# A four-layer graph network on one core: VectorE operations split at 512 columns on gathered tiles, and a rearranged start for the first graph

## The chip, the core and the metric

The kernel runs on one core of one Trainium2 chip. The metric is device time in microseconds, from 14 runs of the kernel before: median 3405.66, lowest 3397.34, highest 3418.8. One further execution was recorded by the profiler; all durations in the text come from that one.

## The reference

There are 16 graphs of 1024 nodes with 64 features each. `adj` is a weighted adjacency matrix (1024 x 1024, about one entry in 128 set, plus the diagonal), `nodemask` a flag for each node. Four layers run one after the other on the features `x`, each on a normalised input and with its result added to `x`:

```
h = max(layernorm(x), 0)
0: x += (adj @ h) @ W^T
1: m = relu(relu(h W1 + b1) W2 + b2);  msg = relu(adj @ m);  x += GRU(msg, h)
2: T0 = h, T1 = adj @ h, T2 = 2 adj @ T1 - T0;  x += (sum of K_k T_k) Wc + bc
3: neighbours = adj > 0; rows of more than 10 neighbours (where the mask is set) drop every skip-th one, in both directions
   agg = 0.25 q(0.25) + 0.5 q(0.5) + 0.25 q(0.75), each q a quantile over the neighbours' h, feature by feature
   x += (relu((h + agg) M1 + mb1) M2 + mb2) * mask
```

## The kernel before

Only the class `Fast` runs on these inputs; a second path (`general_kernel`) is there for inputs that it cannot hold. Engines are called by letters in the code: `T` is TensorE (PE), `V` VectorE (DVE), `S` ScalarE (ACT), `G` GpSimd (POOL), `D` SyncE (SP). All operations of the main part are recorded through one helper, so most of them show as L301 in the profile; the gathers are L622, stores through SP L628, scatters L1288.

**Tiles.** Nodes of a graph lie on 128 partitions in 8 blocks (`NT` = 8), so a feature tile is 128 x 512 in fp32, a block of the adjacency matrix 128 x 8 x 128 (512 KB). `pay` holds for each node x, the normalised h, its list of neighbours, counts and its mask; `G` holds up to 11 gathered neighbours per node (its own row and 10 more), `net` the scratch of the sorting network; there are two `G` buffers and one `net`.

**Chains.** The work is written as generators ("chains") that yield one operation at a time:

- `transposing` (L845): loads blocks of `adj` by SP, transposes them on PE, copies them to `AT` tiles on ACT. There are 15 `AT` tiles, 8 per graph. The first graph's eight blocks are loaded at the start, six of them into parts of the `G` buffers, which are not yet in use.
- `coding` (L652): signs of the `AT` tiles on ACT (`there`, fp16), the diagonal cleared on DVE, and a product on PE with powers of two, which packs a node's neighbours into code words.
- `listing` (L635): loads the node mask, casts and transposes it once; then for each graph turns code words into lists of neighbours with MAX8 and MATCH_REPLACE on DVE (`cand`, `L`, `hit`), and applies the dropping rule.
- `layering` (two chains, even and odd graphs): `layers` (L895) with layers 0 to 2, and the fourth norm. `norm` (L879) sums a row of x on DVE (`st`), takes eight squares with accumulation on ACT (`sq`, `va`), a root on ACT (`sd`), a reciprocal and an offset on DVE (`ri`, `off`), and eight ReLUs with scale and offset on ACT. The product of layer 0 (`into`) follows on PE, block by block. At the end the list goes into `pay` ("pay fill"), the fourth norm writes its h, and SP stores `pay` in DRAM: as `table` (h alone, for the gathers) and as `rows`.
- `gathering`: for each graph 80 indirect DMAs issued by POOL (10 neighbours x 8 blocks, 128 rows each) into a `G` buffer. After graph 16 four more groups follow, for nodes with more neighbours (`MANY`: 1, 2, 4 and 2 blocks of 128 nodes with 23, 15, 13 and 13 entries).
- `quantiling`: on the gathered tile, marks repeated entries (`hits`, `bad`), adds 1e30 to them, sorts with min/max networks (`tensor_tensor` on `G` and `net`), and weighs the wanted places with `coef`.
- `dense`: the sum of the weighed places and the last two products on PE, the mask on DVE (`yo`), the store of the output.

**The width of a VectorE operation.** A network step acts on several places at once. `quantiles` cuts it so that no operation has more than `LONGEST` = 1024 columns: with T = 8 blocks and C = 64 features a place has 512 columns, so `few` is 2 places. The mask addition and the multiplication by `coef` are cut in the same way.

```python
few = max(1, int(LONGEST / (T * C)))

def parts(k):
    count = -(-k // few)
    return [slice(k * i // count, k * (i + 1) // count) for i in range(count)]
```

**The order.** A planner (`Weave.run`, L440) gives every operation an estimated cost (`Line.cost`, L304) and issues, at each step, on the engine that can start earliest, the ready operation of the chain with the lowest key. The keys make graph b's transposes (b - 2.5) and layers (b - 3) run ahead of its lists (b - 1.5), gathers and quantiles (b + 1). The order on each engine is then fixed as a dependence from one instruction to the next, so each engine runs its instructions in the planner's order, whatever their real times are. A change of any operation or cost therefore can change the order of all that follows.

Of the kernel before, what the change touches and what calls it, by code (L numbers as in the profile page):

```python
# [16 lines left out]
AF = mybir.ActivationFunctionType  # L17
ALU = mybir.AluOpType
AX = mybir.AxisListType
# [3 lines left out]
P = 128  # L23
N = 1024
NT = N // P
# [76 lines left out]
GATHER = 1.33  # L102
RANK = 3.0
SHARE = 3
LONGEST = 1024
AT = 15
LIST_KEY = -1.5
CODE_KEY = -2
# [177 lines left out]
class Line:  # L286
# [15 lines left out]
        return op  # L302

    def cost(self, method, out, reads, kwargs):  # L304
        n = max(a.free_size() for a in [out] + reads)
        extra = "accum_out" in kwargs
        if self.name == "DVE":
            fixed = {"match_replace": 0.27, "max": 0.16}.get(method, 0.155)
            return fixed + n / 960 + 0.08 * extra, 0.0
        if self.name == "ACT":  # L310
            scalars = sum(hasattr(kwargs.get(k), "ap") for k in ("bias", "scale"))
            return 0.225 + n / 1400 + 0.09 * scalars + 0.19 * extra, 0.0
        if self.name == "PE":
            if method == "transpose":
                return 0.12, 0.25
            n = out.free_size()
            if n == NB and mybir.dt.size(reads[0].dtype) == 2:
                return 0.12, 0.3
            pair = n == 512 and reads[0].shape[0] == P and out.shape[0] == C
            return (0.46 if pair else max(0.22, 0.06 + n / 545)), 0.3  # L320
        if self.name == "SP":
            return 0.4, 2.0 + out.nbytes() / 150e3
        return 1.33, 2.2


class Weave:
# [16 lines left out]
    def give(self, name, t):  # L343
        self.stocks[name].append(t)
# [121 lines left out]
class Fast:  # L466
# [4 lines left out]
    def __init__(self, tc, half, whole, weights):  # L471
# [93 lines left out]
        self.weave = weave = Weave(tc)  # L565
        self.T, self.V, self.S = Line("PE", nc.tensor), Line("DVE", nc.vector), Line("ACT", nc.scalar)
        self.G, self.D = Line("POOL", nc.gpsimd), Line("SP", nc.sync)
        self.take = {}
        weave.leash = None, None

# [64 lines left out]
    def listing(self, nodemask):  # L635
        V = self.V
        mf, mu8 = self.small("h1", (P, 512))[:, 0:P], self.small("h1")[:, P:2 * P].bitcast(U8)[:, 0:P]
        yield self.D.dma_start(mu8, nodemask.rearrange("b (t p) -> (b t) p", p=P))
        yield V.tensor_copy(mf, mu8)
        bank = yield "q"  # L640
        yield self.T.transpose(bank[:, 0:P], mf, self.ident)
        self.mask = self.small("mask", (P, P))
        yield V.tensor_copy(self.mask, bank[:, 0:P])
        self.weave.give("q", bank)
        for b in range(GRAPHS):
            yield float(b) + LIST_KEY
            yield from self.lists(b)
        yield float(GRAPHS) - RANK
        yield from self.longest()

    def coding(self):

        V, T, S = self.V, self.T, self.S
        for b in range(GRAPHS):
            yield float(b) + CODE_KEY
            bank = yield "bits"
            yield T.matmul(bank.rearrange("p (t w) -> p t w", w=NB), self.ones16[0:1, 0:P],
                           self.low[0:1, None, :].to_broadcast([1, NT, NB]), start=True, stop=False)
            turned = self.turned[b]
            for j in range(0, NT, 2):  # L660
                there = yield "there"
                for i in range(2):
                    yield lambda: len(turned) > j + i
                    yield S.activation(there[:, i, :], turned[j + i], AF.Sign)
                self.masked[b] = j + 2
                own = there.rearrange("p i (t m) -> p (i t) m", m=P)[:, j:j + NT + 2:NT + 1, :]
                yield V.tensor_mul(own, own, self.noteye[:, None, :].to_broadcast([P, 2, P]))
                for i in range(2):
                    for t in range(NT):
                        yield T.matmul(bank[:, t * NB:(t + 1) * NB], there[:, i, t * P:(t + 1) * P],  # L670
                                       self.bits[:, (j + i) * NB:(j + i + 1) * NB], start=False,
                                       stop=j + i == NT - 1 and t == NT - 1)
                self.weave.give("there", there)
            code = yield "code"
            yield S.activation(code.rearrange("p t w -> p (t w)"), bank, AF.Copy, scale=1.0 / UNIT)
            self.weave.give("bits", bank)
            self.coded[b] = code
# [167 lines left out]
    def transposing(self, adj):  # L845

        D, T, S = self.D, self.T, self.S
        blocks = {}


        early = self.early

        def load(i):
            b, j = divmod(i, NT)
            blocks[i] = block = early.pop(0).rearrange("p (t m) -> p t m", m=P) if 2 <= i < NT else (yield "block")
            yield D.dma_start(block, adj[b, :, j * P:(j + 1) * P].rearrange("(t p) m -> p t m", p=P))

        total = GRAPHS * NT
        yield -1.0
        for i in range(NT):  # L860
            yield from load(i)
        for i in range(total):
            b, j = divmod(i, NT)
            yield float(b) - 2.5
            if NT <= i + 1 < total:
                yield from load(i + 1)
            block = blocks.pop(i)
            at = yield "AT"
            for half in range(2):
                bank = yield "tp"  # L870
                for q in range(4):
                    yield T.transpose(bank[:, q * P:(q + 1) * P], block[:, 4 * half + q, :], self.ident)
                yield S.activation(at[:, 512 * half:512 * half + 512], bank, AF.Copy)
                self.weave.give("tp", bank)
            if not 2 <= i < NT:
                self.weave.give("block", block)
            self.turned[b].append(at)

    def norm(self, w, h, X, then=None):  # L879

        V, S = self.V, self.S
        st, va, sd, ri, off = (self.small(f"{name}{w}") for name in ("st", "va", "sd", "ri", "off"))
        yield V.tensor_reduce(st, X, axis=AX.X, op=ALU.add)
        yield V.tensor_scalar(st, st, -1.0 / C, None, op0=ALU.mult)
        sq = self.small(f"sq{w}", (P, C))
        for t in range(NT):
            yield S.activation(sq, X[:, t, :], AF.Square, bias=st[:, t:t + 1], accum_out=va[:, t:t + 1])
        yield S.activation(sd, va, AF.Sqrt, bias=self.eps, scale=1.0 / C)
        yield V.reciprocal(ri, sd)
        yield V.tensor_mul(off, st, ri)  # L890
        for t in range(NT):
            yield S.activation(h[:, t, :], X[:, t, :], AF.Relu, bias=off[:, t:t + 1], scale=ri[:, t:t + 1])
            if then:
                yield from then(t)

    def layers(self, w, b, x):
# [10 lines left out]
        def into(bank, h, last=False):  # L907

            def step(j):
                if j == 0:  # L910
                    yield lambda: len(turned) > 0
                yield lambda: len(turned) > j
                for half in range(2):
                    yield T.matmul(bank[half * C:(half + 1) * C, :], h[:, j, :], turned[j][:, cols[half]],
                                   start=j == 0, stop=not last and j == NT - 1)
                if last:
                    yield lambda: self.masked[b] > j
                    give("AT", turned[j])
            return step
# [10 lines left out]

        h = yield "nodes"
        bank = yield "fm"
        yield from self.norm(w, h, X, into(bank, h))
        self.turns += 1
        wide = yield "wide"
        aggT = wide[0:C, :]
# [15 lines left out]
        def turn(t):  # L952
# [3 lines left out]
            if t % 4 == 3:  # L956
                yield S.activation(cat[0:C, cols[t // 4]], turned_h[-1][0:C, :], AF.Copy)
                give("fm", turned_h[-1])
        yield from self.norm(w, h, X, turn)
        aug = yield "wide"  # L960
        for half in range(2):
            bank = yield "fm"
# [57 lines left out]

        h = yield "nodes"
        bank = yield "fm"
        yield from self.norm(w, h, X, into(bank, h))
        wide = yield "wide"
        t1 = wide[0:C, :]
        for half in range(2):
# [21 lines left out]
                yield T.matmul(both[half * C:(half + 1) * C, t * P:(t + 1) * P], h[:, 4 * half + t, :], self.k02,  # L1048
                               start=False, stop=t == 3)
        give("nodes", h)  # L1050
        aug = yield "wide"
        for half in range(2):
            yield S.activation(aug[0:C, cols[half]], both[half * C:(half + 1) * C, :], AF.Copy)
        give("fm", both)
        bank = yield "fm"
        o = yield from by_node(bank, aug[0:C, :], self.wca, self.bcr)
        give("wide", aug)
        yield V.tensor_add(X, X, o)
        give("fm", bank)


        yield lambda: b in self.listed
        L, notes = self.listed[b]
# [6 lines left out]
                              op0=ALU.mult, op1=ALU.add)  # L1070
        give("L", L)
        give("notes", notes)
        yield from self.norm(w, pay[:, :, H:H + C], X)
        table = self.table[b * STRIDE:b * STRIDE + N, :].rearrange("(t p) c -> p t c", p=P)
        yield self.store(b, "table", table, pay[:, :, H:H + R])
        rows = self.rows[b * N:(b + 1) * N, :].rearrange("(t p) w -> p t w", p=P)
# [870 lines left out]
```

## Time and profile before

| | us |
|---|---|
| median of 14 runs | 3405.66 (3397.34 to 3418.8) |
| the profiled execution | 3409.64 |
| its span (first to last recorded work) | 3407.7 |
| busy: PE | 1783.7 (52%) |
| busy: VectorE | 1548.1 (45%) |
| busy: POOL | 1432.6 (42%) |
| busy: ACT | 1095.1 (32%) |
| first gather starts | 161.2 |
| gathers of graphs 1, 2, 3, 4 (from 0) start | 352.1, 552.8, 745.5, 930.7 |
| gather of the last graph starts | 3035.1 |
| the four groups after it | 3156.2 to 3362.8 |

The mean granted clock of TensorE was 0.656. No engine is busy for more than 52% of the span, so the bound is not read from busy shares; one has to see which engine waits for which, stage by stage. In the page's second part each digit is the busy share of one fortieth of the span (85 us) in tenths. In the part with groups, a line gives the source line, engine, operation, output <- inputs and count, then the busy time and the mean of one in ns, then the idle time of that engine just ahead of these operations and what ended most of it. A line of waits gives the idle time in total, how often, and the longest. On the timelines, consecutive operations of one name are put together: start, time, and "x3" for three; shapes are those of the row. SPq and POOLq are the sequencers, where DMA issues show. In a table of windows each engine's busy time and count stand for one stretch, then the granted clock, the DMA engines' share and the GB/s.

### The profile page before, as it was taken

How to read it: one execution, taken by the hardware profiler on the slowest of the kernel's cores; microseconds unless marked ns; L12 is line 12 of the kernel's file. 1: busy time of each engine (PE TensorE's matmuls, PEld its weight loads, DVE VectorE, ACT ScalarE, POOL GpSimd, SP SyncE). 2: the span in 40 equal slices, each digit the busy share in tenths (PEclk: the TensorE clock that was granted, in tenths of full speed). 3: DMA queues.
4: the chain of work that ended last, by engine and by line, in shares of the span. 5: the costliest groups of instructions: out<-in, count | busy, mean ns of one | idle time of the engine just before them, and what ended most of it. 6: DMA issues, size and time to landing. Idle time of an engine off the chain costs nothing. (4 is left out here: it accounts for less than half of the span.)

```text
span 3407.7 us, 24102 instructions
## 1 busy us (share of the span) xinstructions
PE 1783.7 (52%) x7024; PEld 818.6 (24%) x7024; DVE 1548.1 (45%) x3675; ACT 1095.1 (32%) x3002; POOL 1432.6 (42%) x1441
## 2 busy tenths in 40 slices
PE   6727355382736547282836646581836666433222
PEld 3302112140313223131413212230412232111121
DVE  2212136271725436271725436371725436395846
ACT  5503324160515234151614224250614334111100
POOL 1070623517071634526170634426061534437674
PEclk8857568575777667585767666575766667655555
DMA  3211322222212212222312112221212221112110
GB/s 83 60 27 49 46 43 52 35 63 27 62 31 54 45 30 61 31 51 30 75 25 52 39 31 51 45 58 25 69 25 39 41 38 25 18 21 28 24 29 15
DMA packets 246841, 141.00 MB, mean 41 GB/s; under 512 B 76048, under 2 KB 223952, under 8 KB 246704
## 3 DMA queue, kind: packets, MB, share of 16 engines
q1 hardware_dynamic: 199824, 90.21, 11.0%
q0 software_dynamic: 46096, 48.62, 10.6%
q8 instruction: 59, 0.97, 0.1%
q10 hardware_dynamic: 784, 0.57, 0.1%
q14 instruction: 78, 0.64, 0.1%
HBM read 120.12 MB, written 19.17 MB: 41 GB/s over the span
## 5 line engine op out<-in xcount | busy, mean ns | idle before, releaser
L622 POOL DMA_INDIRECT G<-table,pay x1402 | 1401.0, 999 | 1923.0 <-DVE net L301 1185.9
L301 PE MATMUL bank<-AT,nodes 128*64 128x512 f32 x2048 | 624.7, 691 | 118.6 <-issue 65.9
L301 PE MATMUL bank<-G,c 128*128 128x512 f32 (+3 forms) x382 | 202.5, 653 | 158.6 <-DVE G L301 158.2
L301 PE MATMUL bank<-wide,wg 64*64 64x512 f32 (+1 forms) x192 | 121.9, 721 | 301.7 <-ACT wide L301 301.6
L301 PEld LDWEIGHTS bank<-AT,nodes 128*64 128x64 f32 x2048 | 161.2, 154 | 428.7 <-issue 306.0
L301 PE MATMUL bank<-c,block 128*128 128x128 f32 x976 | 234.2, 371 | 18.1 <-ACT AT L301 8.2
L301 ACT ACTIVATE wide<-bank 64x512 f32<-64x512 f32 x128 | 75.7, 591 | 477.9 <-remote 340.4
L301 DVE MAX8 L<-cand 128x8 f16<-128x103 f16 x384 | 92.3, 263 | 275.1 <-remote 178.4
L301 PE MATMUL bank<-of_h,m 64*128 64x512 f32 (+2 forms) x72 | 62.3, 960 | 280.6 <-issue 227.1
L301 ACT ACTIVATE sq<-pay,st 128x64 f32<-128x64 f32 x512 | 177.7, 347 | 93.3 <-DVE st L301 78.2
L301 ACT ACTIVATE AT<-bank 128x512 f32<-128x512 f32 x256 | 150.2, 590 | 164.5 <-PE bank L301 116.6
L301 PEld LDWEIGHTS bank<-c,block 128*128 128x128 f32 x976 | 155.9, 190 | 171.1 <-issue 140.2
L301 DVE TENSOR_TENSOR G<-G 128x1024 f32<-128x1024 f32 (+7 forms) x215 | 187.4, 902 | 2.2
L301 DVE TENSOR_TENSOR hn<-nodes,bank 128x256 f32<-128x256 f32 x32 | 13.4, 419 | 378.6 <-remote 297.4
L301 DVE SCALAR_TENSOR_TENSOR of_h<-bank,bhn,wide 64x512 f32<-64x512 f32 x32 | 23.8, 744 | 351.3 <-PE bank L301 197.4
L301 PE MATMUL bank<-m,h 128*128 128x64 f32 x274 | 69.0, 410 | 203.6 <-ACT h L301 179.6
L301 ACT ACTIVATE nodes<-pay,off,ri 128x64 f32<-128x64 f32 x384 | 153.5, 429 | 26.8 <-DVE off L301 16.2
L301 DVE TENSOR_TENSOR net<-G 128x1024 f32<-128x1024 f32 (+7 forms) x140 | 140.4, 1032 | 3.2 <-PE bank L301 2.1
L301 PEld LDWEIGHTS bank<-G,c 128*128 128x128 f32 x382 | 74.1, 240 | 272.9 <-issue 150.4
L301 ACT ACTIVATE G<-G,coef 128x64 f32<-128x64 f32 x384 | 95.2, 336 | 127.9 <-DVE coef L301 127.9
L301 ACT ACTIVATE there<-AT 128x1024 f16<-128x1024 f32 x128 | 132.4, 1045 | 0.4
L301 PEld LDWEIGHTS bank<-m,h 128*128 128x128 f32 x274 | 59.7, 308 | 256.0 <-ACT h L301 190.8
(188 smaller groups left out, 2631.0 us busy)
## 6 DMA issues: line engine op xcount, KB each, us to landing
block<-in_adj SPq DMA_DIRECT2D x122, 512.0 KB
G<-table,pay POOLq DMA_INDIRECT x1402
rows<-pay SPq DMA_DIRECT2D x16, 632.0 KB
table<-pay SPq DMA_DIRECT2D x16, 264.0 KB
pay<-in_x SPq DMA_DIRECT2D x16, 256.0 KB
out<-yo SPq DMA_DIRECT2D x16, 256.0 KB
G<-in_adj SPq DMA_DIRECT2D x6, 512.0 KB
c<-in_half ACTq DMA_DIRECT2D x1, 246.0 KB
```

Source lines behind the costliest of these rows:

```text
L301: return Op(self, lambda: f(*args, **kwargs), writes, reads, cost, later)
L622: return self.nc.gpsimd.indirect_dma_start(out=out, out_offset=None, in_=table, in_offset=bass.IndirectOffsetOnAxis(ap=at, axis=0))
```

## The change

Six things are changed.

1. `LONGEST` is 512, so `few` is 1 for the 16 graphs: mask, network and coefficient operations have at most 512 columns. The instructions on VectorE rise from 3406 to 3984 in the built program.
2. A second name for ACT's queue, `self.A`; the odd-numbered blocks of the first graph are loaded by ACT, the even-numbered ones by SP. The planner's cost of a DMA goes by the operation and no longer by the engine.
3. The cast of the node mask waits until the first graph is coded.
4. The coding of words waits until the first graph's product of layer 0 has been issued (`turns > 0`).
5. `norm` has a second form, used for the first graph's four norms: the rows are centred on VectorE, squared and reduced there, the root stays on ACT, and one VectorE operation does the ReLU and the scaling. The eight squares and the eight ReLUs on ACT go (32 and 32 in four norms).
6. For all graphs, the pay fill (which waits for the list) stands ahead of the last part of layer 2 (the copies `aug`, the product by node, the addition to x).

```diff
-LONGEST = 1024
+LONGEST = 512
...
     def cost(self, method, out, reads, kwargs):
+        if method == "dma_start":
+            return 0.4, 2.0 + out.nbytes() / 150e3
...
-        if self.name == "SP":
-            return 0.4, 2.0 + out.nbytes() / 150e3
...
+        self.A = self.S
...
         yield self.D.dma_start(mu8, nodemask.rearrange("b (t p) -> (b t) p", p=P))
+        yield lambda: 0 in self.coded
         yield V.tensor_copy(mf, mu8)
...
             yield float(b) + CODE_KEY
+            yield lambda: self.turns > 0
             bank = yield "bits"
...
-            yield D.dma_start(block, adj[b, :, j * P:(j + 1) * P].rearrange("(t p) m -> p t m", p=P))
+            queue = self.A if i % 2 and i < NT else D
+            yield queue.dma_start(block, adj[b, :, j * P:(j + 1) * P].rearrange("(t p) m -> p t m", p=P))
...
-    def norm(self, w, h, X, then=None):
+    def norm(self, w, h, X, then=None, early=False):
...
+        if early:
+            yield V.tensor_add(h, X, st[:, :, None].to_broadcast([P, NT, C]))
+            square = yield "nodes"
+            yield V.tensor_mul(square, h, h)
+            yield V.tensor_reduce(va, square, axis=AX.X, op=ALU.add)
+            self.weave.give("nodes", square)
+            yield S.activation(sd, va, AF.Sqrt, bias=self.eps, scale=1.0 / C)
+            yield V.reciprocal(ri, sd)
+            yield V.scalar_tensor_tensor(h, h, 0.0, ri[:, :, None].to_broadcast([P, NT, C]), op0=ALU.max, op1=ALU.mult)
+            for t in range(NT):
+                if then:
+                    yield from then(t)
+            return
...
-        yield from self.norm(w, h, X, into(bank, h))
+        yield from self.norm(w, h, X, into(bank, h), early=b == 0)
...
-        aug = yield "wide"
-        for half in range(2):
-            yield S.activation(aug[0:C, cols[half]], both[half * C:(half + 1) * C, :], AF.Copy)
-        give("fm", both)
-        bank = yield "fm"
-        o = yield from by_node(bank, aug[0:C, :], self.wca, self.bcr)
-        give("wide", aug)
-        yield V.tensor_add(X, X, o)
-        give("fm", bank)
-
-
         yield lambda: b in self.listed
         L, notes = self.listed[b]
...
         give("L", L)
         give("notes", notes)
-        yield from self.norm(w, pay[:, :, H:H + C], X)
+
+        aug = yield "wide"
+        for half in range(2):
+            yield S.activation(aug[0:C, cols[half]], both[half * C:(half + 1) * C, :], AF.Copy)
+        give("fm", both)
+        bank = yield "fm"
+        o = yield from by_node(bank, aug[0:C, :], self.wca, self.bcr)
+        give("wide", aug)
+        yield V.tensor_add(X, X, o)
+        give("fm", bank)
+
+
+        yield from self.norm(w, pay[:, :, H:H + C], X, early=b == 0)
```

More of the change, by code (lines that the diff above doesn't have):

```diff
@@ L958, in turn @@
                 give("fm", turned_h[-1])
-        yield from self.norm(w, h, X, turn)
+        yield from self.norm(w, h, X, turn, early=b == 0)
         aug = yield "wide"
@@ L1022, in layers @@
         bank = yield "fm"
-        yield from self.norm(w, h, X, into(bank, h))
+        yield from self.norm(w, h, X, into(bank, h), early=b == 0)
         wide = yield "wide"
```

## The prediction

> **What bounds the kernel now.** I read the page's row of tenths first, then the groups, the waits, and the timelines of POOL and DVE (columns: start, time, engine, line, operation; in brackets the idle time before it and what ended that). The page's "chain that ended last" reaches back only some 55 us, so it says nothing of the other 3350.
>
> ```profile
> DVE  2212136271725436271725436371725436395846
> POOL 1070623517071634526170634426061534437674
> ```
> Where POOL's digit is high, VectorE's is low, and the other way round: the two take turns. The groups and the waits name the turns:
>
> ```profile
> L622 POOL DMA_INDIRECT G<-table,pay x1402 | 1401.0, 999 | 1923.0 <-DVE net L301 1185.9
> ```
> ```profile
> POOL G L622 <- DVE net L301: 1185.9, 15, 100.4
> ...
> DVE hn L301 <- remote: 297.4, 16, 26.8
> ```
> Fifteen times POOL stops for 79 us on average (1185.9/15) until VectorE has done with the G buffer of two graphs earlier. One such stop on POOL's own timeline:
>
> ```profile
> 662.69 0.95 POOL L622 DMA_INDIRECT G<-table,pay  x1 [0.30 <-issue]
> 745.52 1.28 POOL L622 DMA_INDIRECT G<-table,pay  x1 [81.88 <-DVE net L301]
> 747.10 1.43 POOL L622 DMA_INDIRECT G<-table,pay  x1 [0.30 <-issue]
> ...
> 751.59 1.97 POOL L622 DMA_INDIRECT G<-table,pay  x1 [0.30 <-issue]
> ```
> A gather takes 0.95 + 0.30 = 1.25 us, 80 of them 100 us (103 to 110 as seen), then the stop. Gather starts at 745.5 and 3035.1 with 12 graphs between give a **period of 190.8 us**. In the gather the other engines crawl (16 `hn` waits of 297.4/16 = 18.6 us for signals from elsewhere); in the stop VectorE has this much to do:
>
> ```profile
> core 0: us, PE busy (x) PEld busy (x) DVE busy (x) ACT busy (x) POOL busy (x), PEclk, DMA share, GB/s
> 663.00:745.00 82.00, 64.96 (x321) 35.56 (x321) 58.66 (x100) 50.18 (x141) 0.64 (x1) 0.73 0.32 70
> ```
> 58.7 of 82 us: by the rows of that stretch some 42 quantile (mask, network, coefficients), 9 to 11 layers, 2 to 5 the rest of a list, 2 dense and coding. The other 23 are a lag of 5 to 11 us after the last gather and waits on ACT and PE. So a microsecond counts once per period if it lies in the stop or lengthens the gather; beside the gather it costs nothing until it pushes work into the stop. The rest is the start up to 161 us and the tail from 3035 us.
>
> **The start.** SP's queue and VectorE at the beginning:
>
> ```profile
> 2.83 14.39 SPq L301 DMA_DIRECT2D G<-in_adj  x6
> 17.34 2.03 SPq L301 DMA_DIRECT2D h<-in_nodemask  x1
> ```
> ```profile
> 11.96 0.36 DVE L546 COPY wg<-whi_ps 128x192 f32<-128x192 f32 x1 [1.13 <-PE whi_ps L544]
> 23.25 0.23 DVE L301 CAST h<-h 128x128 f32<-128x128 uint8 x1 [10.93 <-DMA h<-in_nodemask]
> 24.04 0.29 DVE L301 COPY mask<-bank 128x128 f32<-128x128 f32 x1 [0.57 <-PE bank L301]
> 24.25 0.19 DVE L301 RECIPROCAL ri<-sd 128x8 f32<-128x8 f32 x1
> ...
> 53.40 0.69 DVE L301 TENSOR_TENSOR pay<-pay,bank 128x512 f32<-128x512 f32 x1 [9.83 <-PE bank L301]
> ```
> The mask's cast, whose load stands behind eight 512 KB blocks, holds VectorE from 12.3 to 23.2. Behind it in VectorE's order wait the reciprocal (its input was there at 12.0), and behind that ACT's eight ReLUs and PE's product, which runs without a gap from 23.8 to 50.6. Four edits act here.
> - **Mask later, norm on VectorE.** The reciprocal can go when x is summed (4.8), centred, squared, reduced (three operations of 0.69, the row of a 512-wide one) and rooted on ACT: about 11 to 12. It no longer sets the product; the blocks do. The first is transposed at 14.0, and a block costs PE 2.8 us (8 transposes, 4 product matmuls, by PE's rows of 24 to 50), so 14.0 + 8 x 2.8 = 36.4 against 50.6: **-14**. The coding of words (0.56 us per block on PE, and ACT's 1.05 us signs) goes behind the product; it is covered by layer 1, since its list is wanted only by the pay fill near 120 (143.5 now, less the gains of this part). If coding ended 15 us later than now, the list's 44 us (66.3 to 110.4 now) would end at 125 and take 5 us back.
> - **Two queues.** Four loads of 0.4 to 2.4 us of issue move to ACT, ahead of its square and root; SP's remaining four and the mask's load come sooner. From 5 to 20 us the 16 engines are busy throughout (267 GB/s at the end), so the last block still lands near 23. I take 0; between -1 and +5 (two more issues of 14.39/6 = 2.4 us ahead of ACT's root, if it became late for the blocks).
> - **Norms 2 and 3.** ACT takes 4.0 us from the sum (54.84) to the reciprocal (59.16), and eight ReLUs of 0.43 (60.0 to 67.7 with the transposes between). On VectorE: 3 x 0.69 + root and reciprocal of about 1.0 + 0.69. **-5**; for norm 3 (115.2 to 119.5 and the 6.2 us before it) **-2.5**.
> - **Norm 4 and the pay fill.** From X's add (142.9) to the table's store (155.5) are 12.6 us: six fill operations (0.7), the sum, ACT's squares (148.2 to 151.9, behind a copy of graph 1 that waits for PE until 147.1), the reciprocal at 152.3, the ReLUs. The fill moves ahead into a wait on PE, and the norm takes some 4 us as above, but its root queues on ACT behind the same copy: **-6**. If the list is late the fill waits for it, and the end of the Chebyshev layer behind it.
>
> The first gather, at 161.2 now,
>
> ```profile
> 161.22 1.03 POOL L622 DMA_INDIRECT G<-table,pay  x1 [144.13 <-DMA table<-pay]
> ```
> comes at about 133 (-28). In the built order graph 1's second norm is planned behind this store and not ahead of it, so it meets the crawl beside gather 0, and gather 1 gives back 3 to 5: **-25**, with ends of -5 (graph 1's table stays at its 347 us) and -33 (nothing given back).
>
> **Splitting at 512 columns.** Rows of both widths:
>
> ```profile
> L301 DVE TENSOR_TENSOR G<-G 128x1024 f32<-128x1024 f32 x97 | 117.4, 1220 | 1.0
> ...
> L301 DVE TENSOR_TENSOR G<-G 128x512 f32<-128x512 f32 x92 | 63.0, 685 | 0.5
> ```
> By busy time a split costs 2 x 685 - 1220 = 150 ns. But neighbours overlap:
>
> ```profile
> 698.39 3.49 DVE L301 SCALAR_TENSOR_TENSOR G<-bad,G 128x1024 f32<-128x1024 f32 x3
> ...
> 716.61 1.29 DVE L301 TENSOR_TENSOR net<-net,G 128x512 f32<-128x512 f32 x2
> ```
> Starts lie (3.49 - 1.22)/2 = 1.137 us apart at 1024, 1.29 - 0.685 = 0.604 at 512. An operation that reads the result just ahead of it starts 0.12 later (1.256, 0.724): 10 of 34 wide ones in a graph now, 5 of 82 afterwards, since halves interleave. Issue per graph: 24 x 1.137 + 10 x 1.256 + 13 x 0.604 + 0.724 = 48.4; then 77 x 0.604 + 5 x 0.724 = 50.1. That is +1.7, 1.4 of it in the stop: **+20** over 13 steady stops and the tail. Ends: 0 (the stop's idle takes it), +85 (566 splits at 150 ns).
>
> [...]
>
> **POOL beside shorter operations.** Beside 1024-wide operations a gather takes 1.28 to 1.97 us and not 0.95 (lines above); the first seven of a steady gather lose 2.6 to 2.9 us. In the tail, beside widths of 256 to 924, they take 1.1 to 1.3. If the excess halves, -1.2 per gather: **-18** over 15. Ends: -40 (all of it), +20 (twice as many operations to meet).
>
> **Lists.** Early norms and moved fills shift what fills VectorE's order. The built order puts 3 to 6 us of list work more behind the second `hn`, inside the stop, for four of eight graphs that I followed; three or four us of waits in the stop (`there`, `yo`, `ri`) can take it, and the waits of ACT's squares are met sooner. I take -1 per stop, **-12**; ends +58 (see below) and -65.
>
> **Tail.** Gather 16 now loses 17 us, and the last four groups 25, beside wide operations; a quarter of it is 11. In the built order two more list blocks of 2.1 us and 1.6 us of splits stand ahead of the release: +6. **-5**, plus or minus 12.
>
> Sum: -25 + 20 - 18 - 12 - 5 = -40. The profiled execution took 3409.6 us (span 3407.7), so 3369.6; the median of the runs is 3405.66, 4.0 lower: **3366**.
>
> **Rivals.**
> - **Lists take the stop (slower, 0.17).** If the pushed list work is not absorbed (+7 in four stops of ten, +2 in the rest), with +1.4 of splits, each stop grows 4.5 us: 13 x 4.5 = +58, less 25 and 5: +28, 3434. It decides from +2.9 per stop (13 x 2.9 = 37 = 30 + 6.8). For it: VectorE's order is fixed, and what stands ahead of the network waits there. Against: 23 us of idle in the stop.
> - **The start is given back (0.20).** Graph 1's table is stored at 346.9 now, at the end of its own crawl beside gather 0; if that does not move, only -15 is left: 3391; with the splits uncovered too, no change. For it: gather 1 waits 90.8 us already. Against: gather 0, which slows that crawl, itself starts earlier.
> - **VectorE gains more (0.15).** If shorter operations let PE and ACT in sooner, -5 per stop and -20 in the tail: -65 - 25 - 20 = -110, 3296. For it: the stop's waits; against: no row shows such a gain.
> - That the two queues do nothing is part of the forecast. [...]
>
> **How the numbers follow.** The forecast has 0.48 and a range of its own of 3340 to 3395. To leave no more than 2 in 10 out, the range reaches to part of the third rival below and to the near part of the first above: 3315 to 3422. A difference of 0.2% (6.8 us) is about what a measurement can tell from none. Faster: 0.48, 0.15, and 0.11 of the second rival, 0.74; same: 0.09 of the second; slower: 0.17.
>
> **What would show it.** First gather near 133 and second near 327; no wait on the mask ahead of the first reciprocal; 512-wide starts 0.604 apart; the mean of a gather below 999 ns; waits on `net` of about 82 us in the steady part; from gather 16 to the end 5 us less. Wrong if the waits on `net` grow by 3 us, or if the second gather stays at 352.

## The result, and the profile after

The changed kernel is **slower**: median 3497.51 us of 10 runs (3482.77 to 3503.25), against 3405.04 of 47 runs of the kernel before; the ratio is 1.0273, 95% interval 1.0253 to 1.0292. I had forecast 3366. The profiled execution took 3510.4 us, 13 us above that median (the profiled one before: 5 us above); its span is 3508.5. The page after, with the row of tenths and the gathers:

```profile
DVE  1413163452717172634535361717254362905745
POOL 1261706244261607062534435170615334262363
...
L623 POOL DMA_INDIRECT G<-table,pay x1402 | 1352.0, 964 | 2033.4 <-DVE net L301 1261.2
```

The two rows still alternate. A gather's mean went from 999 to 964 ns, so POOL has 49 us less to do, and waits 110 us more. A stop on `net` is as long as before (1261.2/16 = 78.8 us), with one more of them. The 49 us are busy time: the thirteen gathers of graphs 2 to 14 took 1419 us from first to last DMA against 1406 before, since POOL waits more inside them (for PE 99 us instead of 46, over the gathers of all graphs). Three stretches, read from POOL's timelines and the spans, say where the time went:

| | first gather | gather of graph 2 | last gather starts | from there to the end |
|---|---|---|---|---|
| before | 161.2 | 552.8 | 3035.1 | 372.6 |
| after | 146.4 | 533.8 | 3041.4 | 467.1 |
| difference of the stretch | -14.8 | -4.2 | +25.3 | **+94.5** |

So the start gained 19.0 us up to graph 2, thirteen periods lost 25.3, and the tail lost 94.5: 100.8 in sum, the difference of the spans. Single traces of one program scatter, so the 25 is a rough number: two traces of `pace_15` (below), which runs the same program up to the last gather, have 2494.5 us for the thirteen periods, 13 less than the changed kernel's trace.

**The tail.** VectorE beside the last gather (3041 to 3144), start, time, operation, and in brackets the idle time ahead of it:

```profile
3068.55 0.72 DVE L301 TENSOR_TENSOR G<-G 128x512 f32<-128x512 f32 x1
3114.62 1.23 DVE L301 TENSOR_TENSOR AT<-AT,c 128x1024 f16<-128x1024 f32 x1 [45.34 <-issue]
...
3154.60 0.42 DVE L301 TENSOR_TENSOR yo<-bank,pay 128x256 f32<-128x256 f32 x1 [37.94 <-remote]
```

In the middle of the network of graph 14 (counted from 0) stands a block of `longest` (`AT`), and later a product of `dense` (`yo`); the rest of the network waits behind them in VectorE's fixed order. What they wait for is seen on PE and ACT:

```profile
3062.29 0.22 PE L301 MATMUL bank<-whose,AT 128*128 128x18 f16 x3
3089.34 0.64 PE L301 MATMUL bank<-c,yo 128*64 128x128 f32 x2 [26.83 <-issue]
```
```profile
3055.51 0.63 ACT L301 ACTIVATE G<-pay 128x528 f32<-128x528 f32 x1
3088.69 0.60 ACT L301 ACTIVATE yo<-bank 128x512 f32<-128x512 f32 x1 [32.56 <-remote]
3111.12 0.59 ACT L301 ACTIVATE of_h<-bank 64x512 f32<-64x512 f32 x1 [21.83 <-remote]
```

PE's last product for `yo` is over at 3062.5; ACT, idle since 3056.1, takes it at 3088.7. **PE's signal came 26 us late**, and the next one, of PE's transposes that ended at 3090.5, 20.6 us. "remote" is how the profile names a release that it cannot tie to an instruction that has just ended. The trace also records the updates of PE's semaphore: between 3058.6 and 3088.7 there are eight, up to 7.7 us apart, for matmuls whose recorded ends are all past by 3062.5; elsewhere an update mostly stands 0.01 to 0.03 us behind its matmul, and ACT starts 0.02 us after the last of the eight. So the update is late, and not ACT. The ends of matmuls in a profile are modelled, so the trace does not tell a signal that was held up from a matmul that finished late; "late signal" below stands for either. In the kernel before, the same steps in the same place took no time to speak of:

```profile
3053.79 0.60 ACT L301 ACTIVATE yo<-bank 128x512 f32<-128x512 f32 x1 [6.63 <-PE bank L301]
```
```profile
3062.23 0.42 DVE L301 TENSOR_TENSOR yo<-bank,pay 128x256 f32<-128x256 f32 x1
```

There ACT followed PE at once and VectorE did not stand. What differs is POOL. The stretch of the last gather, in the kernel before and in the changed one (length; busy us and count of PE, weight loads, VectorE, ACT, POOL; granted clock, DMA share, GB/s):

```profile
3035.00:3152.00 117.00, 51.62 (x178) 25.39 (x178) 76.58 (x114) 19.83 (x62) 92.81 (x80) 0.59 0.19 25
```
```profile
3041.00:3144.00 103.00, 21.42 (x70) 10.00 (x70) 29.67 (x62) 9.02 (x30) 78.52 (x80) 0.55 0.19 26
```

Before, 80 gathers took POOL 92.8 us (30 of them over 1.05 us, most beside 1024-wide operations) and VectorE did 76.6 us of work; after, they took 78.5 at nearly full pace (3 over 1.05), and VectorE got 29.7 done. What it is in those operations that stretched the 30 gathers, the traces do not show.

### The profile page after: what moved, and what is told of

The parts are those of the page before. It is cut to its first block, busy times and chain, and to the rows that moved or that the text cites. A ratio compares the mean times of both kernels' runs of the same rounds, so it can differ in the third digit from the quotient of the medians.

```text
span 3508.5 us, 24567 instructions
## 1 busy us (share of the span) xinstructions
PE 1773.2 (51%) x7024; PEld 802.8 (23%) x7024; DVE 1588.5 (45%) x4253; ACT 1071.9 (31%) x2905; POOL 1381.5 (39%) x1441
## 5 line engine op out<-in xcount | busy, mean ns | idle before, releaser
L623 POOL DMA_INDIRECT G<-table,pay x1402 | 1352.0, 964 | 2033.4 <-DVE net L301 1261.2
L301 PE MATMUL bank<-AT,nodes 128*64 128x512 f32 x2048 | 635.2, 709 | 164.0 <-issue 90.2
L301 PE MATMUL bank<-of_h,m 64*128 64x512 f32 (+2 forms) x72 | 67.2, 1032 | 474.1 <-issue 365.1
L301 PE MATMUL bank<-G,c 128*128 128x512 f32 (+3 forms) x382 | 194.8, 631 | 174.5 <-DVE G L301 174.5
L301 DVE TENSOR_TENSOR G<-G 128x512 f32<-128x512 f32 (+3 forms) x313 | 195.0, 666 | 5.0 <-DVE net L301 1.4
L301 ACT ACTIVATE sq<-pay,st 128x64 f32<-128x64 f32 x480 | 166.6, 347 | 92.4 <-DVE st L301 76.0
L301 DVE TENSOR_TENSOR yo<-bank,pay 128x256 f32<-128x256 f32 (+2 forms) x36 | 14.8, 411 | 374.9 <-remote 151.2
L301 ACT ACTIVATE of_h<-bank 64x512 f32<-64x512 f32 (+2 forms) x36 | 20.4, 566 | 432.7 <-remote 276.1
L301 DVE TENSOR_TENSOR net<-G 128x512 f32<-128x512 f32 (+6 forms) x240 | 147.2, 663 | 7.5 <-remote 4.9
L301 ACT ACTIVATE nodes<-pay,off,ri 128x64 f32<-128x64 f32 x360 | 144.5, 429 | 9.2 <-DVE off L301 6.1
L301 PE MATMUL bank<-c,yo 128*64 128x128 f32 x137 | 34.7, 388 | 203.8 <-issue 172.4
```

The lines of the kernel that those rows point to most:

```text
L301: return Op(self, lambda: f(*args, **kwargs), writes, reads, cost, later)
L623: return self.nc.gpsimd.indirect_dma_start(out=out, out_offset=None, in_=table, in_offset=bass.IndirectOffsetOnAxis(ap=at, axis=0))
```

## Theories and experiments

**A, pace.** When POOL gathers at its full pace (0.95 + 0.30 us), PE's signals come late from some 20 to 30 us on. Wide operations of VectorE slow POOL and so keep the signals on time; halving them takes this brake away. **B, order.** The moved fill, the early norms and more instructions shifted the planned order, and the stops come from that alone. **C, the splits' own time** in the stops.

To measure lateness I took, from the traces, every ACT and VectorE instruction that waits for PE's semaphore and finds its engine idle, and the time from the end of PE's last signalling matmul to its start. A prompt one takes 0.04 us; "late" is over 3.

The experiments ran in five series, each on one chip with the kernel before beside it. On the chips of the result and of three series the kernel before takes 3383 to 3405 us (the "first kind" below), in the other two series 2250 and 2263. Ratios are always to the kernel before of the same series. In the tables, "periods" is the time from the start of graph 2's gather to the start of the last graph's, "tail" the time from there to the end.

**1. Which edit, and where.** `wide_all`: the changed kernel with

```diff
-LONGEST = 512
+LONGEST = 1024
```


> The changed kernel with LONGEST back at 1024; all edits for the first graph and the moved pay fill stay. In the changed kernel the last graph's gather (80 indirect DMAs from 3041) lost almost all of the loss: VectorE stood 45 us ahead of a block of the list of long nodes and 38 us ahead of yo, because PE's signals came 20 to 30 us late, from some 20 us after the gather's start; before, POOL was slowed by 17 us beside the wide operations of the network and the signals came at once. Theory A (pace): 512-wide operations let POOL issue at its full 1.25 us, and this makes PE's signals late; with 1024 the tail from the last graph's gather comes back from 467 to about 373 us, and the start's gain of 15 to 19 us stays: about 3390. Theory B (order): the moved pay fill and the later lists put the blocks behind the signals whatever the width; then it stays near 3490. Theory C (the splits' own cost in the stops, +1.4 us each): 20 less than 3497, about 3478.

`split_only` is the kernel before with the opposite edit, run twice:

> The kernel before with LONGEST at 512 and nothing else. Theory A (pace): the last graph's gather goes wrong as in the changed kernel, some 60 to 95 us, with about 2 us more for each period: 3490 to 3520. Theory B (order from the other edits): only the splits' price and POOL's relief, between -10 and +30 of 3405. Theory C: +20, 3425.

> The kernel before with LONGEST at 512 and nothing else, once more. On a chip like the first: 1.027 again. On a chip with prompt signals: the changed kernel there is 72 us above the same kernel at 1024; if this is the split's price whatever the other edits, 1.02 to 1.035 of before; if the price came from the order that splits and early norms make together, 0.995 to 1.01.

`wide_14` (in the changed kernel) and `narrow_14` (512 in place of 1024, in the kernel before):

```diff
-few = max(1, int(LONGEST / (T * C)))
+few = max(1, int((1024 if c.get("graph") == 14 else LONGEST) / (T * C)))
```


> The changed kernel with 1024-wide mask, network and coefficient operations for one graph only, the one before the last, whose network runs beside the last graph's gather. Theory A (pace): POOL's operations beside it are stretched again (some 30 of the 80 over 1.05 us, 3 in the changed kernel), the signals of PE come at once, and the tail returns by 60 to 95 us: 3400 to 3435. Theory B (order): this edit moves few instructions, so the stop of 45 us stays: 3490 to 3500. Theory C: 2 us less.

> The kernel before, with 512-wide mask, network and coefficient operations for one graph only, the one before the last (the reverse of wide_14). Theory A (pace): beside its network POOL's gathers run at 1.25 us again, PE's signals come late, and the tail loses 50 to 95 us: 3455 to 3500. Theory B (order): the few instructions added change little of the order: 3400 to 3412. A result in between would say that the wide operations of other graphs matter as well.

All on the first kind of chip (but `narrow_14`, below):

| | time | ratio, interval | periods, graph 2 to 15 | tail | late signals (sum) |
|---|---|---|---|---|---|
| before | 3405.04 | | 2482.3 | 372.6 | 47 (767 us) |
| after | 3497.51 | 1.0273, 1.0253 to 1.0292 | 2507.6 | 467.1 | 59 (708) |
| wide_all | 3338.75 | 0.9805, 0.9777 to 0.9833 | 2440.4 | 372.8 | 41 (880) |
| split_only | 3491.36 | 1.0268, 1.0209 to 1.0328 | 2465.8 | 465.9 | 51 (635) |
| split_only_2 | 3488.64 | 1.0254, 1.0232 to 1.0276 | 2473.4 | 467.7 | - |
| wide_14 | 3430.23 | 1.0087, 1.0062 to 1.0111 | 2500.7 | 402.8 | 51 (592) |

Added to the kernel before, the split alone makes a slowdown as large as the whole change's, and all of it in the tail (+93 and +95); the steady part is 9 to 17 us shorter, hardly more than the scatter of single traces. So B, as the effect of the other edits on the tail, falls; and C is too small by far. Wide operations for one graph of 16 give 64 of the tail's 94 us back, and 3430 is what A had said. All edits but the split gain 65 us (`wide_all` against 3403.95 in its series), 50 more than A had said: the tail came back as forecast, and the steady part is 42 us shorter than before, which no theory had. Beside the other edits the split therefore costs 159 us and not 92: of the 172 us between the traces of `wide_all` and the changed kernel, 94 lie in the tail, 67 in the thirteen periods and 10 ahead of graph 2's gather. For the 67 the order that split and other edits make together stays a possible cause; no run separates it. The sum of the late signals over a whole run does not follow the time: it counts where VectorE's order has work behind them.

**2. POOL's pace alone.** `pace_15` leaves VectorE's operations and the planned order of the changed kernel, and adds two useless memsets ahead of each gather of the last graph (the row is overwritten by the gather):

```diff
         def make():
-            return self.nc.gpsimd.indirect_dma_start(
+            last = list(self.weave.last.get(self.G, ()))
+            for _ in range(pace):
+                pre = self.nc.gpsimd.memset(out, 0.0)
+                for o in last:
+                    self.weave.behind(pre, o)
+                last = [pre]
+            ins = self.nc.gpsimd.indirect_dma_start(
```


> The changed kernel with two small memsets of POOL (of the row that is gathered next, 128 x 66) ahead of each of the last graph's 80 gathers, planned at no cost, so that the order on the other engines stays and only POOL's pace falls, by some 0.3 to 0.5 us per gather. Theory A (pace): although POOL has 25 to 40 us more to do, PE's signals come at once during that gather, VectorE's stops of 45 and 38 us go, and the time falls by 30 to 80 us: 3420 to 3470. Theory B (the order alone makes the stops): POOL's extra work comes on top: 3520 to 3540. If it is the width of VectorE's operations and not POOL's pace that keeps the signals on time, also 3520 to 3540.

> The changed kernel with two POOL memsets ahead of each of the last graph's 80 gathers, once more. On a chip like the first it took 33 us less than the changed kernel. On a chip with prompt signals theory A (the slower pace helps only because it keeps PE's signals on time) says that POOL's extra work, 80 x 0.6 to 0.7 = 50 us, comes on top in full or nearly: 30 to 50 us more than the changed kernel (2273 there), 2300 to 2325. If it is as fast or faster there as well, the memsets help by something else.

It took 3464.09 us (1.0185, 1.0165 to 1.0206), and 3456.0 the second time (1.0167, 1.0148 to 1.0186; again on the first kind of chip, so what the memsets do on the second kind stays open here). POOL in that gather, and the stretch:

```profile
3122.86 0.38 POOL L625 MEMSET G<- 128x66 f32 x2
3123.79 0.95 POOL L629 DMA_INDIRECT G<-table,pay  x1 [0.55 <-POOL G L625]
```
```profile
3011.00:3172.00 161.00, 50.56 (x162) 24.27 (x162) 75.93 (x145) 19.82 (x62) 110.26 (x238) 0.56 0.14 20
```

The gather is 59 us longer (1.88 us per gather and more beside VectorE), and yet the tail is 32 us shorter (435.3 against 467.1): none of PE's signals in it was late, and VectorE did 75.9 us of work in its 161 us instead of 29.7 in 103. With VectorE's widths unchanged, this is **POOL's pace and not the width**. B, and the reading that the width itself keeps the signals on time, had 3520 to 3540. A memset could act by more than the pace; that wide operations of VectorE, quite another brake, do the same (`wide_14`) speaks for the pace.

**3. Pace in every gather.** `wide_pace1` has 1024 columns and one memset ahead of each of the 80 gathers of all graphs; `after_pace1` is the changed kernel (512, two queues) with the same memset; `paced_wider` has 1024 columns, one load queue and a memset of four rows (those about to be gathered):

```diff
-                                  reads)
+                                  reads, [whole[:, ((k + 1) * T + t) * R:min((k + 1) * T + t + 4, n * T) * R]] if "graph" in c else ())
```


> The changed kernel with 1024-wide operations, and one memset of POOL (128 x 66) ahead of each of the 80 gathers of all 16 graphs, unplanned. From pace_15 a gather with one memset takes about 1.7 us instead of 1.25, so 36 us more per graph on POOL. Theory A (pace), with late signals in every gather from some 30 us on (first late ones at 28 to 53 us): the work beside a gather gets done, the stops of 79 us shrink by 20 to 45, and the time lies between 3200 and 3500. If slower signals do not limit the steady part (VectorE's work in the stop is fixed by its order), the stops stay at 79 and the time is 3338 + 15 x 36 = 3880 at worst.

> The changed kernel at 1024 with one POOL memset ahead of every gather of the 16 graphs, once more. On the chip with prompt signals it took 1.065 of before. On a chip like the first, where each gather has late signals from some 30 us on: theory A says that the work beside the gathers gets done, stops shrink by 20 to 45 us, and the time is below wide_all's 0.98 of before, between 0.90 and 1.0. If late signals do not limit the steady part, above 1.05.

> The changed kernel as it is (512 columns, two load queues), with one POOL memset (128 x 66) ahead of each of the 80 gathers of the 16 graphs, unplanned. On a chip like the first, without the memset, splitting costs 159 us (3497 against 3339). Theory A (the split is dear because it lets POOL run at full pace): paced, the same split costs less than half of that: 2854 to 2930. If the split is dear for another reason (its own issue time, or its order), the 160 us stay: about 3010. On a chip with prompt signals: 2396 plus 0 to 70.

> The changed kernel at 1024 with one load queue, and one POOL memset of four rows (128 x 264) ahead of each of the 80 gathers of the 16 graphs, unplanned: by wide_pace1_2's 0.17 us for 66 columns and the 2.76 us of a 3168-wide memset, about 0.33 us, so some 1.55 us per gather. On a chip like the first: the late signals' sum falls from 412 us to below 150 and the stops nearly go; POOL then sets 16 x 124 + 133 + 330 = 2450 at best; I expect 2550 to 2750. If the late signals do not fall, 13 us per graph more than 2854, about 3040. On a chip with prompt signals, POOL only has more to do: 2400 to 2560.

On the first kind of chip:

| | us per gather | time | ratio, interval | stops (between gathers), 13 periods | late signals (sum) |
|---|---|---|---|---|---|
| wide_all | 1.25 | 3338.75 | 0.9805, 0.9777 to 0.9833 | 1032 | 41 (880 us) |
| wide_pace1_2 | 1.39 | 2853.88 | 0.8375, 0.8344 to 0.8405 | 460 | 49 (412) |
| after_pace1 | 1.39 | 2793.27 | 0.8274, 0.8219 to 0.8328 | 287 | 32 (240) |
| paced_wider | 1.55 | 2577.13 | 0.7614, 0.7592 to 0.7637 | 8 | 1 (8) |

`paced_wider` is **24% below** the kernel before. Without memsets the same kernel is 2.4% below it (`wide_one_queue_2`, under 5, in another series), so a memset of 0.33 us ahead of each gather takes off some 22%. `paced_wider` lies in the range of its forecast; `wide_pace1_2` and `after_pace1` came out below theirs, the latter with runs from 2740 to 2816. The last one's POOL, and all that is left of "remote" waits on ACT and VectorE:

```profile
1508.05 0.95 POOL L629 DMA_INDIRECT G<-table,pay  x1 [0.27 <-POOL G L625]
1509.00 0.33 POOL L625 MEMSET G<- 128x264 f32 x1
```
```profile
ACT yo L301 <- remote: 9.7, 1, 9.7
DVE net L301 <- remote: 8.2, 1, 8.2
```

In the changed kernel such lines read

```profile
DVE hn L301 <- remote: 302.9, 20, 36.9
ACT of_h L301 <- remote: 276.1, 14, 33.7
```

And once POOL is paced, the split costs nothing: `after_pace1` is below `wide_pace1_2`, though the order of the two differs too and they ran in different series.

**4. Chips without late signals.** Two series ran on them: `narrow_14`, `fill_only`, `one_queue`, `wide_pace1` (before 2250.41), then `after_2`, `wide_all_2`, `fill_only_2`, `wide_one_queue` (before 2262.67). `fill_only` is the kernel before with the pay fill moved as in the change; `one_queue` is the changed kernel with

```diff
-            queue = self.A if i % 2 and i < NT else D
+            queue = D
```
and `wide_one_queue` is `wide_all` with the same edit.

> The kernel before with the pay fill moved ahead of the last part of layer 2 in all graphs, and nothing else. With 1024 the changed kernel's period is 187.7 us against 190.9, and it starts graph 2's gather 29 us sooner. If the moved fill makes the shorter period: 3360 to 3370 (13 periods of 3 us). If the shorter period comes from the other start edits, which change the planned order behind them, it stays at 3400 to 3410.

> The kernel before with only the pay fill moved, once more. On the chip with prompt signals it took 0.985 of before. On a chip like the first: if the moved fill makes the shorter period of wide_all (187.7 us against 190.9), 3360 to 3370; if the other start edits do, 3400 to 3410.

> The changed kernel with all eight loads of the first graph on SP's queue; the planned order of PE, ACT and POOL is the same. In the changed kernel ACT issues its four loads until 18.1 us and only then takes the root (19.4 instead of 12.0), so PE's product starts at 21.0. My forecast had the product start at 14.0 and end at 36.4; it ended at 49.9. If the queue is what failed, the root is at about 12 and the product starts at 14 and ends 6 to 8 us sooner, with the first gather at 138 to 141 instead of 146. If PE's 3.5 us per block sets the end (blocks landing later on one queue), the first gather stays at 145 to 148. The time: 3475 to 3500, since the tail's stops stay.

> The changed kernel once more. The last four runs took place on another chip, where the kernel before takes 2250 us and not 3405, and where none of 300 signals of PE to ACT within the gathers was late by over 1 us (on the first chip 35 of 157 by over 3). If this run is on such a chip: theory A (late signals are what the change made dear) says the change costs little there, within 1% of the kernel before, as the same kernel with one load queue did (2248.6). If it is on a chip like the first: 3497 again.

> The changed kernel with LONGEST at 1024, once more. On a chip like the first: 3339 again (0.98 of before). On a chip with prompt signals: the start is 15 us shorter and the moved fill gains as in fill_only (0.985 of before there), so 0.975 to 0.985 of before; within 0.7% of the changed kernel itself, since the width matters there only by the splits' own cost (30 us at most) and POOL's relief.

> The changed kernel with LONGEST at 1024 and all early loads on SP's queue (the planned order is that of wide_all). With one queue the root came at 9 instead of 19.4 us, the product ended at 39.0 instead of 49.9 and the first gather started at 134 instead of 146. So 9 to 12 us less than wide_all: about 3328 on a chip like the first, and below both kernels; on a chip with prompt signals also 9 to 12 us less than wide_all.

> The changed kernel at 1024 with one load queue, once more. On a chip with prompt signals 0.969 of before. On a chip like the first 9 to 12 us below wide_all's 3339: 0.975 to 0.98 of before.

| | ratio, interval | periods, graph 2 to 15 | tail |
|---|---|---|---|
| after_2 | 1.0043, 1.0013 to 1.0073 | 1564.8 | 344.3 |
| one_queue | 0.9999, 0.9962 to 1.0035 | 1554.6 | 344.2 |
| wide_all_2 | 0.9718, 0.967 to 0.9766 | 1481.4 | 355.9 |
| wide_one_queue | 0.9687, 0.9638 to 0.9735 | 1480.2 | 356.2 |
| fill_only, fill_only_2 | 0.9845, 0.9774 to 0.9916; 0.9852, 0.98 to 0.9904 | 1480.4; 1484.0 | 356.1; 356.7 |
| narrow_14 | 0.9925, 0.988 to 0.9971 | 1508.8 | 345.8 |
| wide_pace1 | 1.0646, 1.057 to 1.0722 | 1644.6 | 369.7 |

Of the 365 to 399 waits on PE in each of the six traces that I measured (without the last two), none was over 0.9 us, though POOL's best pace is the same 1.25 us. There the tail behaves as I had forecast (12 us shorter with 512 columns, where I had put -5, plus or minus 12), and a memset only costs: `wide_pace1` is 6.5% above the kernel before and 9.5% above `wide_all_2`, where on the first kind it was 16% and 15% below them. The sign turns with the late signals, as A says, though the two kinds of chip may differ in more than that. But the split is not free there: 72 us between `after_2` and `wide_all_2`, in the periods (120.4 us against 114.0), more than I expected. So beside the other edits the split can cost some 80 us in the steady part without any late signal, as much as the 67 us on the first kind. POOL's stops are 84 us instead of 7, its waits within the gathers 138 instead of 8. VectorE is busy 40 us longer (1600.0 against 1560.1), which is 2.5 of the 6.4 us per period; what the rest is, order or else, was not tried. `narrow_14` and `fill_only` were to answer questions about the first kind, and those stay open: neither ran there, so which of the other edits makes `wide_all`'s shorter periods is not known. On the second kind the moved fill alone takes off 1.5%, of the 2.8% of `wide_all_2`.

**5. The load queue.** ACT at the start of the changed kernel, and of `one_queue`:

```profile
9.86 8.23 ACTq L301 DMA_DIRECT2D G<-in_adj  x3
18.12 1.28 ACT L301 ACT_TABLE_LOAD   x1 [18.12 <-DMA G<-in_adj]
19.42 0.30 ACT L301 ACTIVATE sd<-va,eps 128x8 f32<-128x8 f32 x1
```
```profile
5.76 1.28 ACT L301 ACT_TABLE_LOAD   x1 [5.76 <-DMA pay<-in_x]
8.95 0.30 ACT L301 ACTIVATE sd<-va,eps 128x8 f32<-128x8 f32 x1 [1.90 <-DVE va L301]
```

With its own loads ahead, ACT issues until 18.1 and takes the root at 19.4 instead of 9.0; PE's product ends at 49.9 instead of 39.0, and the first gather starts at 146.4 instead of 134.3 (145.3 in `after_2`, on the same kind of chip as `one_queue`). So the second queue cost the start 9 to 12 us (first gathers of 144.0 and 145.4 in the two runs of `wide_all`, 135.1 and 133.0 with one queue). On the first kind of chip `wide_one_queue_2` took 3318.43 (0.9759, 0.9732 to 0.9785), the fastest there without memsets, 84 us below the kernel before.

## Why the prediction was wrong

- **Tail, -5: measured +94.5.** The step that failed is "POOL beside shorter operations", and the "quarter of it" that the tail took over from it: I counted POOL's relief as a gain (-18, and -11 in the tail). The relief of busy time came: a steady gather lost 1.0 to 1.7 us beside VectorE instead of 2.6 to 2.9, as forecast, and gather 16 with the last four groups 29 less where I had put 11 (all in all 35 ns x 1402 = 49 us). In the steady part it shortened no gather (1419 us against 1406 for thirteen). In the tail POOL's slowness was what kept PE's signals on time in the only gather that has much of VectorE's work beside it (76.6 us before, against 28.6 in the steady gather from 745 to 850). I had the pieces: that others crawl beside a gather (the `hn` waits of 18.6 us), and that wide operations stretch POOL. I did not ask whether the crawl depends on POOL's pace. The third rival even had shorter operations let PE and ACT in sooner; the opposite is true on this kind of chip.
- **Slower rival.** It had the right sign and the wrong place: list work pushed into the stops, +58 over 13 periods. The periods lost 12 to 25, the tail 94. (Its own working adds up to 0.4 x 7 + 0.6 x 2 + 1.4 = 5.4 us a stop, +70, and not 4.5 and +58.)
- **Splitting, +20.** The pitch held (685 ns, starts 0.604 apart), and on the first kind of chip the split alone left the steady part as it was or 9 to 17 us shorter, within what I had bounded with POOL's relief and the lists. Beside the other edits it made it 67 us longer (`wide_all` to the changed kernel), near the +85 that I had given as the upper end; what makes it so is not shown.
- **Lists, -12.** The steady part lost 12 to 25 us, though the split alone (-9 to -17) and the other edits alone (-42, `wide_all`) each gain. They do not add, since each changes the planned order of all that follows. I can show that they do not, not which instructions make it.
- **The start, -28 and -3 given back.** 14.8 and then 4.2 more, 19.0 in all against 25. Two sizes were off. "Two queues: I take 0" cost 9 to 12 us by the runs; its bound of +5 was too small because I counted two issues of 2.4 us where four, of 0.40, 0.60, 2.13 and 3.03 us from 9.42 on, kept ACT from its table load until 18.1. What made the last two the longest is not shown. And a block costs PE 3.5 us, not 2.8 (the product took from 10.6 to 39.0 in `one_queue`). Without the queue the product ends at 39.0 and the first gather starts at 134.3, against 36.4 and 133 as worked out: the chain of steps was right, the closeness partly luck, since the product began 3.4 us sooner than the 14.0 that I had put and took 6 us longer. Norm 2 gained 5 as I said (from X's add to the next product 8.3 us instead of 13.3). The coding ended at 94 instead of 63, and the list at 129.4, as the step "if coding ended 15 us later" feared, twice as late; the pay fill waited for it. Nothing was given back at gather 1.
- **Readings of the profile before.** Two were a little off, without weight in the sum. The fifteen waits of 79 us on average are fourteen stops of 84 us and one short wait after the last gather; and 267 GB/s is the mean up to 17 us, where the row from 10 to 20 us has 283.
- **Median and chip.** The forecast was made for the chip of the profile, where the kernel loses 2.7%; on the other kind the same change costs 0.4%. The profile of one chip could not show that.

## What to carry to other kernels

An engine that gets faster off the critical path can make others slower: here POOL's gathers of the last graph took 78.5 us instead of 92.8, and the tail grew by 94.5. Before an edit relieves an engine, look at the stretches in which that engine is *slowed now* and see what works only there. Waits that end in "remote", long after the engine that they wait for has finished, can be a cost of their own (26 us for one of ACT in the last gather here); measure the time from the signal's end to the wait's end beside each engine's pace. A DMA issued by an engine with work in its order can hold that work up: four loads kept ACT from 9.4 to 18.1 us here. And a cure found on one chip may cost on another: the memset that took off 15 to 22% on one kind added 9.5% on the other.

## What the runs showed of the hardware that I had not expected

- On one kind of chip, PE's signals arrive late while POOL issues an indirect DMA each 1.25 us, by up to 65 us in the kernel before; at 1.39 us the latest took 24 us (the late ones sum to 412 and 240 us instead of 880), at 1.55 us one of 368 was late. What carries the signals and why the pace matters is open. Of the waits on VectorE's signals that found ACT or PE idle, 1 of 151 was over 3 us late in the kernel before and none of 148 in the changed one; of those on ACT's signals that found VectorE idle beside the gathers before, 13 of 59 look late by over 3 us, 8 of them of operations that wait for PE as well.
- Two chips ran the same program in 2250 and 2263 us instead of 3383 to 3405, with no late signal. Whether that is the chip or a state that it was in, and which kind is the rule, can't be told from five series.
- The late signals do not begin at once: in 15 of the 16 gathers before, the first signal that came late was given 18 to 55 us in, in the changed kernel 8 to 40 us in. In the last gather before, which the wide operations slowed, none of the first 90 us was late.
